# An adjacency product moved into a gap of the q products, and a new order for the first loads and norms

## The chip, the cores and the metric

The kernel runs on one core of one Trainium2 chip. Its time is the device time in microseconds, the median of several runs; the kernel before takes 1536.66 us (1535.83 to 1537.0 in three runs). One more run was profiled; its trace spans 1534.6 us, and every time of a single instruction here is counted from the start of that span.

The engines are named by what they do: TensorE (PE, matmuls; PEld, its weight loads, which can overlap matmuls), VectorE (DVE), ScalarE (ACT), GpSimd (POOL) and SyncE (SP, which here only issues DMA transfers).

## The reference, cut to what matters

128 matrices x of 128 x 512 go through two layers. The first takes the norm of the rows, multiplies by an adjacency matrix and adds the row maximum to x. The second is an attention over 8 heads of 64 with projections q, k and v, in which only pairs count whose adjacency is not zero.

```python
# layer 0
h = jnp.maximum(_layernorm(x, axis=-1), 0.0)
A = jnp.einsum('od,bdn->bon', W1, x)                    # W1 = W2 = adj, x = h
C = jnp.einsum('od,bdn->bon', W2, x) + b[None, :, None]
pre = A[:, :, None, :] + (C - A)[:, :, :, None]
out = jnp.max(jax.nn.relu(pre), axis=-1)                # added to x
# layer 1
h = jnp.maximum(_layernorm(x, axis=-1), 0.0)
q = (x @ Wq + bq).reshape(b, n, H, HD)                  # k and v alike, x = h
scores = jnp.einsum('bihd,bjhd->bhij', q, k) / jnp.sqrt(jnp.float32(HD))
mask = jnp.where(adj == 0, jnp.float32(-1000000000.0), jnp.float32(0.0))
weights = jax.nn.softmax(scores + mask[None, None, :, :], axis=-1)
out = jnp.einsum('bhij,bjhd->bihd', weights, v)         # added to x
```

Because both weights of layer 0 are adj, its output is one number for each row: the maximum of a row of adj @ h, plus a bias, cut at zero. Adding one number to a whole row does not change that row's norm, so the kernel norms each matrix once and uses h in both layers.

## The kernel before

The 128 matrices are worked in 32 groups of four. For each group, q, k and v are formed by a fast matrix product after Strassen and Winograd: seven products (p1 to p7) of half-size blocks of h and of the weights in place of eight. Two of them, p4 and p3, are split once more in the same way (p43a, p43b), except in the first and last group's v. The first group's q is formed in the plain way (`plain_q`). Its results are collected in PSUM banks, read out by ScalarE (`biased`) or added by VectorE.

The norm of one matrix m: statistics on VectorE, two small operations on GpSimd, the rest on ScalarE.

```python
def norm(m):
    ...                                                          # cut: HT, AMAX, C of a new group
    HN[m] = work.tile([P, N], F32, name="hn", bufs=3)
    nc.vector.bn_stats(st, x_of(m))                              # L276
    nc.vector.bn_aggr(mv, st)
    nc.vector.tensor_scalar_add(ve, mv[:, 1:2], EPS)
    nc.gpsimd.tensor_tensor(rstd, ve, mhalf, op=ALU.pow)         # L281
    nc.gpsimd.tensor_scalar(nmr, mv[:, 0:1], rstd, -1.0, op0=ALU.mult, op1=ALU.mult)

def norm_end(m):
    nc.scalar.activation(HN[m], x_of(m), AF.Relu, scale=RSTD[m], bias=NMR[m])   # L286
    if m >= G:
        add_bv(m)                                                # GpSimd, L292
```

h is needed transposed. The first group's four matrices are transposed on TensorE (`transposes`, L318, read out by ScalarE); later ones in 32 x 32 blocks on VectorE (`blocks`, L299), whose blocks 16 small DMA transfers for each pair of matrices then put in place (`move`, L309).

```python
def adjacency(m):
    g, i = divmod(m, G)
    pa = bank(7)
    nc.tensor.matmul(pa, adjT, HN[m], start=True, stop=True)     # L324
    nc.vector.reduce_max(AMAX[g][:, i : i + 1], pa, axis=AX.X)   # L325
    ...                                                          # cut: C of a full group
```

`h_sum` (L342) forms the four sums of blocks of h, `h_blocks` (L351 to L353) and `weight_blocks` (L366) those for the split products, `weight_sums` (L378) those of the weights. The products, cut to what waits for what:

```python
def p1(self):
    self.mm(self.a, "a11", "b11", True)              # eight matmul instructions, L415
    ...                                              # v: one copy on ScalarE
    for f in range(2):
        self.biased(self.pf[f], self.a, f)           # ScalarE, L430: p1a, then u

def p6(self):
    self.mm(self.b, "s2", "t2", True)
    nc.vector.tensor_tensor(self.u[:, 1], self.b, self.pf[0], op=ALU.add)    # L454

def p2(self):
    self.mm(self.a, "a12", "b21")                    # adds into the bank of p1
    self.biased(self.dst(0, 0), self.a, 0)

def p7(self):
    self.mm(self.b, "s3", "t3")                      # adds into the bank of p6
    nc.vector.tensor_tensor(self.u3, self.b, self.pf[1], op=ALU.add)         # L463

def p5(self):
    self.mm(self.c, "s1", "t1", True)
    self.add(self.dst(1, 1), self.c, self.u3)        # L436

def p43b(self):
    for k in range(2):
        self.block_mm(scr[:, 0, k], s[:, k, 2], t[:, k, 2])      # small matmuls, L481
    self.more(u[:, :, 0, 1], scr[:, 0])                          # VectorE, L484
    ...                                                          # cut: 12 instructions into other banks
    for k in range(2):
        self.block_mm(scr[:, 0, k], s[:, k, 1], t[:, k, 1])      # scr again
    ...                                                          # cut: L484 twice, L436 twice
```

The whole is scheduled by hand: each engine works in the order in which its instructions are written. A group's turn is `apply` of the group before (L594), `scores` (L564, read out by ScalarE, L572), then 18 steps: v (steps 0 to 5), q of the next group (6 to 11) and k of the next group (12 to 17), each as p1, p6, p2, (p7, p43a), p5, p43b. After each step other work is put in by a table. `next_norms` is the part for the group after next:

```python
def next_norms(m):
    return {
        0: [(norm_end, m), (norm, m + 1), (norm_end, m + 1)], 4: [(blocks, m)],
        8: [(norm, m + 2), (norm_end, m + 2), (adjacency, m)],
        9: [(blocks, m + 1), (move, m + 1)],
        12: [(norm, m + 3), (norm_end, m + 3), (adjacency, m + 1)],
        13: [(blocks, m + 2)],
        14: [(blocks, m + 3), (move, m + 3), (adjacency, m + 2)],
    }
```

The beginning:

```python
nc.scalar.dma_start(adj_sb, adj)
...
for i in range(G):
    (nc.scalar if i > 0 else nc.sync).dma_start(x_of(i), x[i])
load_w(nc.sync, "q", 0)
load_w(nc.sync, "q", 1)
nc.scalar.activation(live[:, 0:1], mhalf, AF.Copy)
for name in "kv":
    load_w(nc.sync, name, 0)
    load_w(nc.scalar, name, 1)
...                                       # cut: biases on GpSimd's queue, three loads of x, adjT
for m in range(G):
    norm(m)
    norm_end(m)
    if m in (1, 2):
        transposes(m - 1)
    if m == 2:
        adjacency(0)
nc.vector.tensor_single_scalar(live, adjT, 0.0, op=ALU.not_equal)
transposes(2)
adjacency(1)
transposes(3)
adjacency(2)
adjacency(3)
weight_sums(nc.gpsimd, "v")
plain_q(0, 0)
plain_q(0, 1)
weight_sums(nc.vector, "k")
for k in range(4):
    h_sum(0, k)
norm(G); norm_end(G); norm(G + 1); norm_end(G + 1)
plain_q(1, 0)
blocks(G); blocks(G + 1); move(G + 1)
plain_q(1, 1)
...                                       # k of group 0, p1 p6 p2 p7 p5 p4 p3, with other work between
weight_sums(nc.gpsimd, "q")
```

Of the kernel before, what the change touches and what calls it, by code (L numbers as in the profile page):

```python
# [52 lines left out]
P = 128  # L53
G = 4
# [113 lines left out]
def tile_adj_preln_d2(  # L168
# [38 lines left out]
    def fast(ctx):  # L207
# [11 lines left out]
        def bank(k):  # L219

            return ps.tile([P, 512], F32, name=f"bk{k}")

        def x_of(b):
            return X[b // 2][:, b % 2, :]
# [6 lines left out]
        def load_w(eng, name, h):  # L231
            src = dict(q=wq, k=wk, v=wv)[name]
            eng.dma_start(
                W[name][:, 2 * h : 2 * h + 2, :],
                src[2 * h * P : (2 * h + 2) * P].rearrange("(c p) f -> p c f", p=P),
            )
# [3 lines left out]
        for p in range(2):  # L240
            X[p] = xpool.tile([P, 2, N], F32, name="xp")
        for i in range(G):
            (nc.scalar if i > 0 else nc.sync).dma_start(x_of(i), x[i])
        load_w(nc.sync, "q", 0)
        load_w(nc.sync, "q", 1)
        nc.scalar.activation(live[:, 0:1], mhalf, AF.Copy)
        for name in "kv":
            load_w(nc.sync, name, 0)
            load_w(nc.scalar, name, 1)
        nc.gpsimd.dma_start(b0_sb, b0.rearrange("(p o) -> p o", o=1))  # L250
        nc.gpsimd.dma_start(bq_sb, bq.rearrange("(c p) -> p c", p=P), allow_slow_non_contiguous=True)
        nc.gpsimd.dma_start(bk_sb, bk.rearrange("(c p) -> p c", p=P), allow_slow_non_contiguous=True)
# [13 lines left out]
        def norm(m):  # L266

            g, i = divmod(m, G)
            if i == 0:
                HT[g] = proj.tile([P, G, NC, D], F32, name="hT")  # L270
                AMAX[g] = stat.tile([P, G], F32, name="amax")
                C[g] = stat.tile([P, G], F32, name="c")
            HN[m] = work.tile([P, N], F32, name="hn", bufs=3)
            st = stat.tile([P, 6], F32, name="st")
            mv = stat.tile([P, 2], F32, name="mv")
            nc.vector.bn_stats(st, x_of(m))  # L276
            nc.vector.bn_aggr(mv, st)
            ve = stat.tile([P, 1], F32, name="ve")
            nc.vector.tensor_scalar_add(ve, mv[:, 1:2], EPS)  # L279
            rstd = RSTD[m] = stat.tile([P, 1], F32, name="rstd")  # L280
            nc.gpsimd.tensor_tensor(rstd, ve, mhalf, op=ALU.pow)  # L281
            nmr = NMR[m] = stat.tile([P, 1], F32, name="nmr")
            nc.gpsimd.tensor_scalar(nmr, mv[:, 0:1], rstd, -1.0, op0=ALU.mult, op1=ALU.mult)  # L283
# [36 lines left out]

        def adjacency(m):
            g, i = divmod(m, G)
            pa = bank(7)
            nc.tensor.matmul(pa, adjT, HN[m], start=True, stop=True)  # L324
            nc.vector.reduce_max(AMAX[g][:, i : i + 1], pa, axis=AX.X)  # L325
            if i == G - 1:
                nc.vector.tensor_scalar(C[g], AMAX[g], b0_sb, 0.0, op0=ALU.add, op1=ALU.max)
# [54 lines left out]
        def weight_sums(eng, n):  # L382
            for k in range(4):
                weight_sum(eng, n, k)
# [254 lines left out]
        def next_norms(m):  # L639

            return {
                0: [(norm_end, m), (norm, m + 1), (norm_end, m + 1)], 4: [(blocks, m)],
                8: [(norm, m + 2), (norm_end, m + 2), (adjacency, m)],
                9: [(blocks, m + 1), (move, m + 1)],
                12: [(norm, m + 3), (norm_end, m + 3), (adjacency, m + 1)],
                13: [(blocks, m + 2)],
                14: [(blocks, m + 3), (move, m + 3), (adjacency, m + 2)],
            }

        with tc.manual_schedule():  # L650

            for m in range(G):
                norm(m)
                norm_end(m)
                if m in (1, 2):
                    transposes(m - 1)
                if m == 2:
                    adjacency(0)
            nc.vector.tensor_single_scalar(live, adjT, 0.0, op=ALU.not_equal)
            transposes(2)  # L660
            adjacency(1)
            transposes(3)
            adjacency(2)
            adjacency(3)
            weight_sums(nc.gpsimd, "v")
            plain_q(0, 0)
            plain_q(0, 1)
            weight_sums(nc.vector, "k")
            for k in range(4):
                h_sum(0, k)  # L670
            norm(G)
            norm_end(G)
            norm(G + 1)
            norm_end(G + 1)
            plain_q(1, 0)
            blocks(G)
            blocks(G + 1)
            move(G + 1)
            plain_q(1, 1)
            k = Products(0, "k")  # L680
            more = {
                0: [(adjacency, G), (norm, G + 2), (norm_end, G + 2)],
                1: [(norm, G + 3), (norm_end, G + 3), (blocks, G + 2)],
                2: [(adjacency, G + 1)], 3: [(blocks, G + 3), (move, G + 3)],
                4: [(adjacency, G + 2)], 5: [(adjacency, G + 3)],
            }
            for s, p in enumerate((k.p1, k.p6, k.p2, k.p7, k.p5, k.p4, k.p3)):
                p()
                for f, m in more.get(s, ()):
                    f(m)  # L690
            weight_sums(nc.gpsimd, "q")
            for g in range(NG):
                b = g * G
                if g > 0:
                    apply(g - 1)
                scores(g)
                part = []
                for p in [Products(g, "v")] + [Products(g + 1, n) for n in "qk" if g + 1 < NG]:
                    part += [[p.p1], [p.p6], [p.p2]]
                    if p.n == "v" and g in (0, NG - 1):  # L700
                        part += [[p.p7], [p.p5], [p.p4, p.p3]]
                    else:
                        part += [[p.p7, p.p43a], [p.p5], [p.p43b]]
                todo = {s: [] for s in range(len(part))}

                def add(s, *what):
                    todo[s].append(what)

                m = b + 2 * G
                if g + 1 < NG:  # L710
                    if g > 0:
                        for i in range(G):
                            residual(b - G + i)
                    if m < B:
                        norm(m)
                    if 0 < g < NG - 1:
                        add(0, adjacency, m - 1)
                    for k, s in enumerate((1, 2, 2, 3)):
                        add(s if g > 0 else 3, h_sum, g + 1, k)
                    for k, s in enumerate((6, 7)):  # L720
                        add(s, h_blocks, g + 1, k)
                    if g + 2 < NG:
                        for s, l in next_norms(m).items():
                            for what in l:
                                add(s, *what)
                    else:
                        add(6, count, 0, b)
                    eng = nc.gpsimd if m < B else nc.vector
                    for k, s in enumerate((8, 9, 9, 10, 10, 13, 14, 15)):
                        add(s, mask, eng, b + k // 2, k % 2)  # L730
                    if g + 2 < NG:
                        add(0, load, 2 * g + 5)
                    if g + 3 < NG:
                        add(8, load, 2 * g + 6)
                else:
                    for k, s in enumerate((0, 0, 0, 0, 2, 2, 3, 4)):
                        add(s, mask, nc.vector, b + k // 2, k % 2)
                    for i, s in enumerate((0, 0, 0, 1)):
                        add(s, residual, b - G + i)
                if g == 0:  # L740
                    add(0, weight_blocks, nc.gpsimd, "q")
                    add(8, weight_blocks, nc.gpsimd, "k")
                    for i in range(G):
                        add(15, add_bv, i)
                    add(15, weight_blocks, nc.gpsimd, "v")
                for s, ps_ in enumerate(part):
                    for p in ps_:
                        p()
                    for f, *args in todo[s]:
                        f(*args)  # L750

            g = NG - 1
            apply(g, 2)
            count(B - 2 * G, B)
            for i in range(G):
                residual(g * G + i, nc.gpsimd if i < 2 else nc.vector)
            pc = bank(1)
            for k in range(2):
                nc.tensor.matmul(pc[0:1, 0:1], CNT[k], ones, start=k == 0, stop=k == 1)
            nc.scalar.copy(flag, pc[0:1, 0:1])  # L760
# [38 lines left out]
```

## Time and profile before

| engine | busy us | share of the span |
|---|---|---|
| TensorE, matmuls | 1513.8 | 99% |
| TensorE, weight loads | 1322.7 | 86% |
| VectorE | 1158.9 | 76% |
| GpSimd | 600.1 | 39% |
| ScalarE | 426.8 | 28% |

A matmul that stands waiting counts as busy in this table, so 99% does not mean that TensorE is never held up; the spacing of equal pieces of work shows that better. The trace counts matmul instructions as they are executed: a matmul of these 32-bit numbers appears as two, so a product p1 of four matmuls as eight. Back to back the eight take 1.73 us, an adjacency product of two instructions 0.86 us.

The chain of waits is the work that ended last, followed back from the end: a piece of it is work that nothing released later than the piece before. The timeline lists the instructions of all engines in order of time, with the idle time ahead of each and what ended it in brackets.

### The profile page before, as it was taken

Reading aid. Unit: us, or ns where it says so; the run is one execution under the profiler, and the core shown is the slowest. Engines: PE = TensorE matmul, PEld = TensorE weight load, DVE = VectorE, ACT = ScalarE, POOL = GpSimd, SP = SyncE. Lnnn points to the kernel's source line nnn. Section 1 sums busy time; section 2 is a strip of 40 time slices with the busy share of each in tenths; the row PEclk is TensorE's granted clock in tenths of the full one; section 3 lists DMA queues with packets and bytes.
Section 4 is the critical chain, followed back from the end, with each engine's and each line's share of the span. In section 5 each row is a group of like instructions: output and inputs, shape, how many; then the busy total and the mean of one; then the engine's idle time right before and its main releaser. Section 6 shows DMA issues by size and latency. Waiting matters only on the chain.

```text
span 1534.6 us, 32745 instructions
## 1 busy us (share of the span) xinstructions
PE 1513.8 (99%) x12909; PEld 1322.7 (86%) x12909; DVE 1158.9 (76%) x2485; ACT 426.8 (28%) x844; POOL 600.1 (39%) x670
## 2 busy tenths in 40 slices
PE   7999999999999999999999999999999999999997
PEld 5888888888888888888888888888888888888887
DVE  5677777777787777777777877777777777777776
ACT  3223232322232232322322322323223222222221
POOL 4574443243432444423434324344234343243400
PEclk9999999999999999999999999999999999999999
DMA  4233122331222321223312223212233122232111
GB/s 165 51 83 84 26 73 72 81 83 38 65 74 75 84 68 42 72 72 81 84 38 65 72 76 84 62 45 73 73 83 84 29 72 73 77 84 50 44 34 57
DMA packets 307803, 105.28 MB, mean 69 GB/s; under 512 B 273152, under 2 KB 273280, under 8 KB 307648
## 3 DMA queue, kind: packets, MB, share of 16 engines
q1 hardware_dynamic: 306352, 101.00, 25.3%
q8 instruction: 103, 1.69, 0.5%
q10 hardware_dynamic: 1120, 1.90, 0.4%
q14 instruction: 52, 0.43, 0.1%
q0 software_dynamic: 176, 0.27, 0.1%
HBM read 37.03 MB, written 33.55 MB: 46 GB/s over the span
## 4 chain that ended last, share of the span: by engine, by line
PE 97%; DVE 1%; SPq 1%; DMA 1%; issue 0%; POOL 0%; ACT 0%; DVEq 0%; ACTq 0%
PE bk L415 54%; PE bk L481 19%; PE bk L594 8%; PE bk L564 8%; PE bk L324 7%; PE bk L540 1%; SPq L309 1%; DMA xp<-in_x_dram 1%; DVE hs L342 0%; DVE o L612 0%; DVE amax L325 0%; DVE v L436 0%; PE bk L318 0%; ACT hn L286 0%; DVE st L276 0%
## 5 line engine op out<-in xcount | busy, mean ns | idle before, releaser
L281 POOL TENSOR_TENSOR rstd<-ve,mhalf 128x1 f32<-128x1 f32 x128 | 70.7, 552 | 719.4 <-DVE ve L279 719.4
L576 POOL TENSOR_TENSOR w<-w,live 128x512 f32<-128x512 f32 x240 | 297.5, 1272 | 0.0
L484 DVE TENSOR_TENSOR u<-u,bk 128x256 f32<-128x256 f32 x552 | 205.9, 415 | 115.3 <-PE bk L481 111.1
L572 ACT ACTIVATE w<-bk 128x512 f32<-128x512 f32 x256 | 128.9, 624 | 362.7 <-PE bk L564 362.7
L292 POOL TENSOR_TENSOR xp<-xp,bv_sb 128x512 f32<-128x512 f32 x128 | 165.7, 1296 | 118.3 <-ACT hn L286 118.3
L415 PEld LDWEIGHTS bk<-hs,sk_sb 128*128 128x128 f32 x768 | 143.6, 190 | 44.7 <-issue 29.2
L415 PE MATMUL bk<-hs,sk_sb 128*128 128x256 f32 x768 | 181.3, 379 | 0.0
L415 PE MATMUL bk<-sv_sb,hs 128*128 128x256 f32 x768 | 181.2, 379 | 0.0
L415 PE MATMUL bk<-hs,sq_sb 128*128 128x256 f32 x744 | 175.9, 379 | 0.1
L415 PEld LDWEIGHTS bk<-sv_sb,hs 128*128 128x128 f32 x768 | 143.6, 190 | 31.1 <-issue 14.3
L415 PEld LDWEIGHTS bk<-hs,sq_sb 128*128 128x128 f32 x744 | 138.9, 190 | 30.9 <-issue 14.3
L286 ACT ACTIVATE hn<-xp,nmr,rstd 128x512 f32<-128x512 f32 x128 | 104.2, 814 | 161.3 <-POOL nmr L283 161.3
L324 PE MATMUL bk<-hn,adjT 128*128 128x512 f32 x256 | 131.8, 596 | 0.8 <-DVE amax L325 0.8
L463 DVE TENSOR_TENSOR u<-bk,u 128x512 f32<-128x512 f32 x95 | 65.7, 692 | 88.1 <-PE bk L415 85.5
L325 DVE TENSOR_REDUCE amax<-bk 128x1 f32<-128x512 f32 x128 | 88.2, 689 | 52.8 <-PE bk L324 51.9
L594 PE MATMUL bk<-v,w 128*64 128x65 f32 x4096 | 126.6, 222 | 0.0
L594 PEld LDWEIGHTS bk<-v,w 128*64 128x64 f32 x4096 | 122.1, 137 | 4.1 <-issue 0.3
L415 PE MATMUL bk<-wv_sb,hT 128*128 128x256 f32 x512 | 124.3, 386 | 0.0
L564 PE MATMUL bk<-qT,kT 64*128 64x128 f32 x2048 | 122.9, 275 | 0.0
L415 PE MATMUL bk<-hT,wk_sb 128*128 128x256 f32 x512 | 121.1, 379 | 0.0
L415 PE MATMUL bk<-hT,wq_sb 128*128 128x256 f32 x496 | 120.5, 386 | 0.0
L564 PEld LDWEIGHTS bk<-qT,kT 64*128 64x128 f32 x2048 | 116.8, 188 | 2.5 <-issue 0.3
(148 smaller groups left out, 2353.5 us busy)
## 6 DMA issues: line engine op xcount, KB each, us to landing
out_dram<-o SPq DMA_DIRECT2D x128, 256.0 KB, 2.4
xp<-in_x_dram SPq DMA_DIRECT2D x62, 512.0 KB, 4.9
hT<-tb SPq DMA_DIRECT2D x992, 32.0 KB, 1.9
wq_sb<-in_L_gnn_Wq_dram SPq DMA_DIRECT2D x2, 512.0 KB, 6.3
xp<-in_x_dram ACTq DMA_DIRECT2D x3, 256.0 KB, 6.8
wk_sb<-in_L_gnn_Wk_dram SPq DMA_DIRECT2D x1, 512.0 KB, 11.1
wv_sb<-in_L_gnn_Wv_dram SPq DMA_DIRECT2D x1, 512.0 KB, 12.2
wk_sb<-in_L_gnn_Wk_dram ACTq DMA_DIRECT2D x1, 512.0 KB, 9.8
```

What stands on the lines that cost most here:

```text
L281: nc.gpsimd.tensor_tensor(rstd, ve, mhalf, op=ALU.pow)
L286: nc.scalar.activation(HN[m], x_of(m), AF.Relu, scale=RSTD[m], bias=NMR[m])
L292: nc.gpsimd.tensor_tensor(x_m, x_m, bv_sb, op=ALU.add)
L324: nc.tensor.matmul(pa, adjT, HN[m], start=True, stop=True)
L325: nc.vector.reduce_max(AMAX[g][:, i : i + 1], pa, axis=AX.X)
L415: nc.tensor.matmul(bank[:, r, :], lhs, rhs, start=first and r == 0 and c == 0, stop=r == 1 and c == 1, skip_group_check=True,)
L481: nc.tensor.matmul(out, lhs, rhs, start=start, stop=True, skip_group_check=True)
L484: nc.vector.tensor_tensor(to, to, what, op=ALU.add)
L564: nc.tensor.matmul(psc[j][:, f, :], KT[g][r, f, i * D : (i + 1) * D], QT[g][r, f, i * D : (i + 1) * D], start=True, stop=True,)
L572: nc.scalar.activation(w[:, j], psc[j], AF.Exp, scale=HD ** -0.5)
L576: eng.tensor_tensor(w[:, j], w[:, j], live_h, op=ALU.mult)
L594: nc.tensor.matmul(pav[r, c : c + HE], w[:, h % 2, h // 2, r], V[:, i, h, :], start=True, stop=True,)
```

## The change

It moves work; no matmul is added or removed.

- In the turn of a group, the adjacency product of the group after next's first matrix goes from behind q's third product (p2) to between q's second (p6) and third, where p2 has to wait until the bank of p1 has been read out. The block transposition of the same matrix goes from behind v's p5 to behind q's p2.
- At the beginning, the first four matrices and all weights are loaded by one queue, x first. The first group's h is written into the output tile O[0], which is not needed until later, so that four norms need no free hn buffer. Two banks take its adjacency products in turn, and the order of norms, transpositions, adjacency and plain q products is new.
- In group 0 two of the four h sums go two and one steps later, and q's weight blocks are formed ahead of the group's turn. In group 30, the masks that VectorE applies get other steps.

```diff
         for i in range(G):
-            (nc.scalar if i > 0 else nc.sync).dma_start(x_of(i), x[i])
-        load_w(nc.sync, "q", 0)
-        load_w(nc.sync, "q", 1)
+            nc.sync.dma_start(x_of(i), x[i])
         nc.scalar.activation(live[:, 0:1], mhalf, AF.Copy)
-        for name in "kv":
-            load_w(nc.sync, name, 0)
-            load_w(nc.scalar, name, 1)
+        for name in "qkv":
+            for h in range(2):
+                load_w(nc.sync, name, h)
...
-            HN[m] = work.tile([P, N], F32, name="hn", bufs=3)
+            if m < G:
+                if m == 0:
+                    O[0] = one.tile([P, G, N], F32, name="o")
+                HN[m] = O[0][:, m]
+            else:
+                HN[m] = work.tile([P, N], F32, name="hn", bufs=3)
...
-            pa = bank(7)
+            pa = bank(7 if g > 0 else 5 + i % 2)
...
-                0: [(norm_end, m), (norm, m + 1), (norm_end, m + 1)], 4: [(blocks, m)],
-                8: [(norm, m + 2), (norm_end, m + 2), (adjacency, m)],
+                0: [(norm_end, m), (norm, m + 1), (norm_end, m + 1)],
+                7: [(adjacency, m)], 8: [(norm, m + 2), (norm_end, m + 2), (blocks, m)],
...
             for m in range(G):
                 norm(m)
-                norm_end(m)
-                if m in (1, 2):
-                    transposes(m - 1)
-                if m == 2:
-                    adjacency(0)
+                if m < 2:
+                    norm_end(m)
+            transposes(0)
+            transposes(1)
+            norm_end(2)
+            norm_end(3)
             nc.vector.tensor_single_scalar(live, adjT, 0.0, op=ALU.not_equal)
+            adjacency(0)
+            adjacency(1)
             transposes(2)
-            adjacency(1)
             transposes(3)
-            adjacency(2)
-            adjacency(3)
             weight_sums(nc.gpsimd, "v")
             plain_q(0, 0)
+            adjacency(2)
             plain_q(0, 1)
+            adjacency(3)
             weight_sums(nc.vector, "k")
...
             weight_sums(nc.gpsimd, "q")
+            weight_blocks(nc.gpsimd, "q")
...
-                    for k, s in enumerate((1, 2, 2, 3)):
-                        add(s if g > 0 else 3, h_sum, g + 1, k)
+                    for k, s in enumerate((1, 2, 2, 3) if g > 0 else (3, 3, 4, 5)):
+                        add(s, h_sum, g + 1, k)
...
-                    for k, s in enumerate((8, 9, 9, 10, 10, 13, 14, 15)):
+                    at = (8, 9, 9, 10, 10, 13, 14, 15) if m < B else (4, 8, 8, 12, 12, 13, 14, 14)
+                    for k, s in enumerate(at):
                         add(s, mask, eng, b + k // 2, k % 2)
...
-                    add(0, weight_blocks, nc.gpsimd, "q")
```

## The prediction

> **What bounds the kernel now.** I read the page first, for the engine that is full and for the chain that ended last.
>
> ```profile
> PE 1513.8 (99%) x12909; PEld 1322.7 (86%) x12909; DVE 1158.9 (76%) x2485; ACT 426.8 (28%) x844; POOL 600.1 (39%) x670
> PE 97%; DVE 1%; SPq 1%; DMA 1%; issue 0%; POOL 0%; ACT 0%; DVEq 0%; ACTq 0%
> ```
>
> TensorE sets the end nearly everywhere, at a clock granted at nine tenths or more in all 40 slices. The change removes no matmul, so all it can win is time in which TensorE waits. The list of waits shows little of that under PE, but one entry under the weight loads comes back in every group of four matrices:
>
> ```profile
> PEld bk L415 <- ACT u L430: 12.5, 32, 0.4
> ```
>
> (engine, line, what it waited for: us in total, times, longest). Because busy time includes a matmul that stands waiting for its weights, I then took the chain of waits piece by piece, for a late, undisturbed group (start, duration, what):
>
> ```profile
> 1419.03 5.18 PE bk L415 x24
> ...
> 1426.83 2.42 PE bk L481 x20
> 1429.25 5.45 PE bk L415 x24
> 1434.70 0.86 PE bk L324 x2
> ...
> 1439.90 2.23 PE bk L481 x20
> ```
>
> Equal work takes unequal time here. Twenty-four instructions of products one to three take 5.18 us, but 5.45 for q. Twenty small ones of the split products take 2.23 for q and k, but 2.42 for v. So q's first three products lose 0.26 us (5.44 or 5.45 against 5.18; I take 0.26) and v's small products 0.19 us in each group. The chain shows the same pair of excesses throughout, group after group, 47.02 us apart (236.95, 283.97, 330.98 for the score products). The timeline of the same group shows the two causes:
>
> ```profile
> 1427.48 0.70 DVE L299 STREAM_TRANSPOSE tb<-hn 128x512 f32<-128x512 f32 x1
> ...
> 1428.10 0.38 DVE L484 TENSOR_TENSOR u<-u,bk 128x256 f32<-128x256 f32 x1
> ...
> 1428.54 0.71 PE L481 MATMUL bk<-ssv_sb,h 128*128 128x128 f32 x4
> ...
> 1431.81 0.85 ACT L430 ACTIVATE u<-bk,bq_sb 128x256 f32<-128x256 f32 x2
> ...
> 1432.70 1.59 PEld L415 LDWEIGHTS bk<-hT,wq_sb 128*128 128x128 f32 x8 [0.40 <-ACT u L430]
> ```
>
> The block transposition (L299) stands on VectorE ahead of the addition L484, which has to empty the scratch bank before v's last four small matmuls may write it: L484 ends at 1428.48, they start at 1428.54. In q the third product adds into the first product's bank, which ScalarE is still reading out into p1a and u; it is done at 1432.66.
>
> For the beginning I read the timeline from 0 to 48 us. From 18.39 us on TensorE works without a break (13.81 us of plain q products, then k's products and four adjacencies) to the score products at 47.66. What stands close behind it is this row of ScalarE work:
>
> ```profile
> 31.56 0.81 ACT L286 ACTIVATE hn<-xp,nmr,rstd 128x512 f32<-128x512 f32 x1 [2.25 <-POOL nmr L283]
> ...
> 32.27 1.55 ACT L547 ACTIVATE qT<-bk,bq_sb 128x256 f32<-128x256 f32 x4
> ...
> 34.70 0.84 ACT L430 ACTIVATE u<-bk,bk_sb 128x256 f32<-128x256 f32 x2
> ...
> 36.36 1.89 PE L415 MATMUL bk<-hT,wk_sb 128*128 128x256 f32 x8
> ```
>
> ScalarE ends u at 35.54, and k's third product starts at 36.36: only 0.8 us of slack. Last, the v products of group 0:
>
> ```profile
> 62.66 0.68 DVE L436 TENSOR_TENSOR v<-bk,u 128x512 f32<-128x512 f32 x1
> ...
> 63.48 1.96 PE L415 MATMUL bk<-sv_sb,hT 128*128 128x256 f32 x8 [1.42 <-DVE v L436]
> ```
>
> **What the Trainium skill says.** "TensorE: Matmul & The Clock Gate", section "Step-by-step: what each phase is for": the queue of TensorE pulls weight loads ahead of running matmuls, the matmuls stay in order. The trace agrees: the loads of a product normally begin 0.2 us before its first matmul; at q's third product they begin with it (1432.70 and 1432.71). Same page, "What's actually happening": the array begins at half clock and is released by activity. Four transpositions take 1.11 us at 6.92 and 0.66 at 11.51. "DMA: Bandwidth & Descriptors", "Issuing engines are not separate DMA queues": transfers of all issuers share the same 16 engines. The trace moves 315 to 406 GB/s in the late slices of the first 20 us, when little but SyncE's own loads is left, so I take one queue to be no slower. "SBUF — State Buffer", "Who interferes with whom": a VectorE instruction with two SBUF inputs and a GpSimd one that reads SBUF block each other. Here such a sum takes 1.64 us instead of 0.68 (at 21.08, beside GpSimd's sums).
>
> **The change, part by part.**
>
> 1. Adjacency between q's second and third product, in groups 0 to 29. The 0.86 us of adjacency is only moved. It starts when the second product ends, about 257.0 in the group I worked on; ScalarE is done with u at 257.12, the third product now starts at 257.9. The wait goes: 30 x 0.26 = 7.8 us.
>
> 2. The block transposition moves from v's fifth product to behind q's third. VectorE then reaches L484 as soon as the matmuls before it end. Groups 1 to 29 (group 0 has no small v products): 29 x 0.19 = 5.5 us. Does it make a wait in its new place? There VectorE must do, from the end of q's second product: L454 0.60 (pitch), h sums 1.0, amax 0.6, statistics 1.0, transposition 0.65, together some 4 us, and is then due at L463 when the fourth product ends. TensorE takes 0.86 + 1.73 + 1.73 = 4.3 us until then. It just fits; before, VectorE stood idle 1.10 us there. I count 0.
>
> 3. Group 0, v: L436 stood behind four h sums. With two of them moved back it can end near 61.1, before the fourth product ends (60.17 + 1.73 = 61.90). The last product starts there instead of 63.48, that is 1.58; I count 1.5.
>
> 4. Group 0, k: before the small k products the chain shows 2.50 us for the twenty instead of 2.23, behind a row hn - add bv - masks and weight blocks on GpSimd - statistics - hn. Part 1 and 2 move amax ahead of the statistics (0.66 us later), while TensorE comes 0.26 earlier. I expect 0.9 us more waiting there, once. Elsewhere GpSimd has 0.5 us of idle time at that place and takes it up.
>
> 5. Group 30: masks on VectorE. q's small products are torn apart there, from 1486.22 to 1489.72 in place of 2.23 us: 1.27 lost. The new places free them, but one mask now stands where the transposition stood in v (0.19). Gain 1.1.
>
> 6. The beginning. All of x goes first, about 1.1 MB with adj; at 0.4 MB per us after some 2.5 us x3 lands near 5.7 (the third and fourth norm started at 8.52 and 11.98 before). The norms then follow each other on VectorE at 1.0 us, ScalarE finishes hn of matrix 3 near 11.2, and TensorE runs from 6.92 with little rest: two cold transpositions 2.2, a cold adjacency 1.7, a warm one 0.9, two transpositions 0.9. The plain q products start near 12.6 instead of 18.39. But two adjacencies now lie between them, VectorE does the k weight sums and h sums only after the fourth amax, and that starts at 12.6 + 2 x (3.45 + 0.86) = 21.2. Then 6.0 us to the norm of matrix 4 (7.94 before, less 1.9 for the collision with GpSimd's sums, which now come earlier), 5.19 to hn of matrix 5 (26.37 to 31.56 before) and 3.7 until ScalarE is done with u (31.56 to 35.54, less 0.25 of waiting for TensorE). k's third product then starts at 36.2, against 36.36. TensorE wins almost 6 us at the start and hands it back in two waits around k's first three products. I count 0.1.
>
> The weight blocks of q on GpSimd end near 51 instead of 64 us; q's second small use of them was not waited for, so nothing. Sum: 7.8 + 5.5 + 1.5 - 0.9 + 1.1 + 0.1 = 15.1 us, 1536.66 - 15.1 = 1521.6.
>
> **The rivals.** (a) The transposition makes a wait of its own behind q's third product, since it fits by only some 0.3 us; VectorE's 76% speak for it, its idle 1.10 us against it. A wait like v's would come back: 30 x 0.19 = 5.7 us lost, 1527.3. (b) The beginning does bring its gain, if VectorE's sums are faster or the plain products start earlier than I think: up to 3.6 us at k's first product (18.39 + 13.81 = 32.20 against 12.6 + 13.81 + 1.72 = 28.1, were nothing else late), so 1518. Against it stands the row of ScalarE shown above. (c) The output tile serves four norms and is followed as one thing: then the first transposition waits for hn of matrix 1 and the first adjacency for hn of matrix 3, the plain products start near 14, and k's third product 1.4 us later than now: 1523. (d) Moving the adjacency moves a wait to q's fourth product, which needs L454: it ends 257.98, and the product starts 259.6. Nothing speaks for it.
>
> **Range and chances.** The two gains per group are read off identical pieces of the trace and are the surest: 13.3 us. The single places add up to 1.8 with an uncertainty of about 3 either way, and rival (a) costs up to 6. So 1517.5 to 1527.5 holds it 8 times in 10. For 2% some 30.7 us would have to go; all waits together don't hold as much. Chances: faster by over 2% 0.02, within 2% 0.97, slower 0.01.
>
> **What would show it.** The distance from one group's score products to the next should fall from 47.02 to 46.57 us; q's three products should read 1.73 + 1.73, an adjacency of 0.86, then 1.73, and v's twenty 2.23. The weight loads' wait for u should drop from 32 entries to two or so. Plain q should start near 12.6, k's third product near 36.2 with a wait for ScalarE ahead of it. A 2.42 in q's twenty would show (a); k's third product at 34 would show (b). If groups stay at 47.02 the reading of the pieces is wrong.

## The result, and the profile after

| | median us | range | runs |
|---|---|---|---|
| before | 1536.55 | 1535.83 to 1537.0 | 5 |
| after | 1521.13 | 1520.77 to 1521.34 | 5 |

The ratio is 0.99, with a 95% interval of 0.9885 to 0.9914: 15.4 us less. The profiled span fell by as much, from 1534.6 to 1519.2 us. First the page of the changed kernel: busy time by engine, then the chain that ended last, by engine.

```profile
PE 1499.8 (99%) x12909; PEld 1323.4 (87%) x12909; DVE 1152.1 (76%) x2485; ACT 426.6 (28%) x844; POOL 597.3 (39%) x670
PE 96%; DVE 2%; POOL 1%; ACT 0%; issue 0%; DMA 0%; DVEq 0%; POOLq 0%; ACTq 0%
```

The number of matmuls is the same, 12909, yet TensorE's busy time fell by 14.0 us. A matmul that waits counts as busy, so nearly the whole gain is waiting that had been hidden in this figure. The list of waits (us in total, times, longest) shows it for the weight loads; before, this entry stood at 32 times:

```profile
PEld bk L418 <- ACT u L433: 4.2, 3, 3.5
```

Line numbers are three higher than before: L418 is the products, L484 the small matmuls, L327 the adjacency. The chain of waits for the same group (start, duration, what; v, then q, then k):

```profile
1412.95 2.23 PE bk L484 x20
1415.18 3.46 PE bk L418 x16
1418.64 0.86 PE bk L327 x2
1419.49 3.45 PE bk L418 x16
...
1425.57 2.23 PE bk L484 x20
```

v's twenty small matmuls take 2.23 us in place of 2.42. q's first two products take 3.46, the adjacency 0.86, and the next two products 3.45: no piece is longer than its like elsewhere. From one group's score products to the next it is 46.57 us (234.40 to 280.96), before 47.02.

The beginning, from the timeline (start, duration, engine, line, tiles, shape; in brackets the idle time ahead and what ended it):

```profile
12.38 3.62 PE L543 MATMUL bk<-hT,wq_sb 128*128 128x256 f32 x16
```

```profile
32.32 0.81 ACT L289 ACTIVATE hn<-xp,nmr,rstd 128x512 f32<-128x512 f32 x1 [2.26 <-POOL nmr L286]
33.04 1.56 ACT L550 ACTIVATE qT<-bk,bq_sb 128x256 f32<-128x256 f32 x4
...
35.18 0.87 ACT L433 ACTIVATE u<-bk,bk_sb 128x256 f32<-128x256 f32 x2
...
36.11 1.99 PE L418 MATMUL bk<-hT,wk_sb 128*128 128x256 f32 x8 [3.14 <-ACT u L433]
```

The plain q products start 5.85 us earlier than before (in the chain of waits at 12.54, against 18.39), and k's third product 0.25 us earlier: TensorE now stands 3.14 us waiting for the row on ScalarE, which in turn waited 2.26 for GpSimd's end of a norm (nmr).

**Where the 15.4 us came from**, read from the starts of score and apply products in both chains:

| stretch | gain us |
|---|---|
| to the scores of group 0 | 0.14 |
| the rest of group 0's turn | 1.06 |
| groups 1 to 29, 29 x 0.453 | 13.14 |
| group 30 | 1.07 |

### The profile page after: what moved, and what is told of

Same layout as the page of the kernel before. It is cut to its first block, busy times and chain, and to the rows that moved or that the text cites. A ratio compares the mean times of both kernels' runs of the same rounds, so it can differ in the third digit from the quotient of the medians.

```text
span 1519.2 us, 32776 instructions
## 1 busy us (share of the span) xinstructions
PE 1499.8 (99%) x12909; PEld 1323.4 (87%) x12909; DVE 1152.1 (76%) x2485; ACT 426.6 (28%) x844; POOL 597.3 (39%) x670
## 4 chain that ended last, share of the span: by engine, by line
PE 96%; DVE 2%; POOL 1%; ACT 0%; issue 0%; DMA 0%; DVEq 0%; POOLq 0%; ACTq 0%
PE bk L418 54%; PE bk L484 19%; PE bk L597 8%; PE bk L567 8%; PE bk L327 7%; PE bk L543 0%; POOL w L579 0%; POOL ssk_sb L369 0%; PE bk L321 0%; DMA xp<-in_x_dram 0%; POOL rstd L284 0%; DVE sk_sb L381 0%; POOL xp L295 0%; DVE hs L345 0%; ACT hn L289 0%
## 5 line engine op out<-in xcount | busy, mean ns | idle before, releaser
L418 PEld LDWEIGHTS bk<-hs,sk_sb 128*128 128x128 f32 x768 | 143.6, 190 | 44.7 <-issue 29.2
L418 PE MATMUL bk<-hs,sk_sb 128*128 128x256 f32 x768 | 181.3, 379 | 0.0
L418 PE MATMUL bk<-sv_sb,hs 128*128 128x256 f32 x768 | 181.2, 379 | 0.0
L418 PE MATMUL bk<-hs,sq_sb 128*128 128x256 f32 x744 | 175.9, 379 | 0.1
L418 PEld LDWEIGHTS bk<-sv_sb,hs 128*128 128x128 f32 x768 | 143.6, 190 | 31.1 <-issue 14.3
L418 PEld LDWEIGHTS bk<-hs,sq_sb 128*128 128x128 f32 x744 | 138.9, 190 | 18.1 <-DVE u L457 0.5
L289 ACT ACTIVATE hn<-xp,nmr,rstd 128x512 f32<-128x512 f32 x124 | 100.9, 814 | 169.1 <-POOL nmr L286 169.0
L327 PE MATMUL bk<-hn,adjT 128*128 128x512 f32 x248 | 126.7, 592 | 0.3 <-ACT hn L289 0.3
L418 PE MATMUL bk<-hT,wk_sb 128*128 128x256 f32 x512 | 121.2, 380 | 3.1 <-ACT u L433 3.1
L418 PE MATMUL bk<-wv_sb,hT 128*128 128x256 f32 x512 | 124.3, 386 | 0.0
L418 PE MATMUL bk<-hT,wq_sb 128*128 128x256 f32 x496 | 117.3, 379 | 0.0
```

The lines of the kernel that those rows point to most:

```text
L418: nc.tensor.matmul(bank[:, r, :], lhs, rhs, start=first and r == 0 and c == 0, stop=r == 1 and c == 1, skip_group_check=True,)
```

## The experiments

The theory: the gain per group is two separate waits of TensorE (for ScalarE's u in q, for VectorE's transposition in v), the beginning gives nothing, and two single places give the rest. The rivals: the beginning does take part in the gain; the two moves need each other; the transposition sits in its new place with no room left.

**The adjacency alone** (before, with the product moved to step 7 and the transposition left in v):

```diff
-                8: [(norm, m + 2), (norm_end, m + 2), (adjacency, m)],
+                7: [(adjacency, m)], 8: [(norm, m + 2), (norm_end, m + 2)],
```

> The kernel before, with the adjacency product alone moved between q's second and third product; the block transposition stays behind v's fifth. My theory (two separate waits): 30 x 0.26 = 7.8 us faster, less 0.7 to 0.9 in group 0 where the statistics move behind the row maximum, so about 1529.6; q's first three products spaced 1.73, 1.73, 0.86, 1.73, v's twenty small matmuls still 2.42. Rival one (both excesses have one cause, the place of the adjacency product): some 12.5 us faster, v's twenty at 2.23. Rival two (what costs is the switch between kinds of products, not the wait): no change, 1536.5.

Measured: 1529.65 us (1529.54 to 1529.89; before on that chip 1536.45), ratio 0.9956, 0.9942 to 0.9969. A group takes 46.75 us, 0.26 less. Its chain (v, then q):

```profile
1374.01 2.42 PE bk L481 x20
1376.43 3.46 PE bk L415 x16
1379.88 0.86 PE bk L324 x2
1380.74 3.45 PE bk L415 x16
```

q's excess is gone, v's 2.42 stays. The moved product removes q's wait by itself and nothing else. In group 0 k's small products wait 0.98 us here (0.18 before), the one cost that was predicted for it.

**The transposition alone** (before, `blocks` at the end of step 8, the adjacency left there):

```diff
-                0: [(norm_end, m), (norm, m + 1), (norm_end, m + 1)], 4: [(blocks, m)],
-                8: [(norm, m + 2), (norm_end, m + 2), (adjacency, m)],
+                0: [(norm_end, m), (norm, m + 1), (norm_end, m + 1)],
+                8: [(norm, m + 2), (norm_end, m + 2), (adjacency, m), (blocks, m)],
```

> The kernel before, with the block transposition alone moved from behind v's fifth to behind q's third product; the adjacency product stays behind q's third. My theory: 29 x 0.19 = 5.5 us faster, about 1531.0; v's twenty small matmuls 2.23, the three q products still 5.44. Rival (the transposition brings its wait along to q): nothing won, v 2.23 but q's twenty 2.42, 1536.5.

Measured: 1531.12 us (1530.74 to 1531.42), ratio 0.9965, 0.9951 to 0.9979; 46.83 us a group, 0.19 less. The mirror image in the chain:

```profile
1375.11 2.23 PE bk L481 x20
1377.34 5.44 PE bk L415 x24
```

0.26 and 0.19 make the 0.45 us that the whole change brings: the two add up, and neither needs the other.

**The beginning alone** (before, with the one queue, the norms into the output tile, the two banks and the new order of the start; nothing else).

> The kernel before, with the new beginning alone (one queue, first h in the output tile, two banks, new order up to the plain q products); groups are worked as before. My theory (the gain is handed back in the wait for ScalarE ahead of k's third product): plain q starts near 12.4 instead of 18.2, k's third product near 36.1 instead of 36.4, time 0.2 us less, 1536.4. Rival (the beginning brings what its plain products win): 3.6 to 5.8 us faster, 1531 to 1533.

Measured: 1537.23 us (1535.61 to 1539.85), ratio 1.0007, 0.9999 to 1.0015: no gain. Its timeline shows the same pair of rows as the changed kernel, a start at 12.38 and a wait that takes it back:

```profile
12.38 3.62 PE L543 MATMUL bk<-hT,wq_sb 128*128 128x256 f32 x16
...
36.12 1.99 PE L418 MATMUL bk<-hT,wk_sb 128*128 128x256 f32 x8 [3.14 <-ACT u L433]
```

v's last product of group 0 still starts 1.59 us after the end of the one before it, so that gain isn't part of the beginning either.

**Two queues again** (after, with the x and weight loads divided between SyncE and ScalarE as before). It asks what the single queue is worth when the start around it is the new one.

```diff
-            nc.sync.dma_start(x_of(i), x[i])
+            (nc.scalar if i > 0 else nc.sync).dma_start(x_of(i), x[i])
+        load_w(nc.sync, "q", 0)
+        load_w(nc.sync, "q", 1)
...
+            load_w(nc.scalar, name, 1)
```

> The changed kernel, with the loads on two queues again as before. My theory: the third and fourth norm start 2 to 4 us later, plain q starts 0.5 to 2 us later, and since the fourth row maximum, the sums and the norm of matrix 4 follow it one for one, k's third product and the end are as much later: 1521.6 to 1523.1. Rival (the loads were never on the way, only the order of work was): no change, 1521.1.

Measured: 1525.15 us (1524.07 to 1525.34), ratio 0.9927, 0.9913 to 0.994; the span is 3.1 us longer than after. The profiled run is the fastest of the five; the other four take another 1 us, and what that is stays open. The third matrix's statistics wait for their data, and everything behind follows:

```profile
10.02 0.69 DVE L281 BATCH_NORM_STATS2 st<-xp 128x6 f32<-128x512 f32 x1 [3.21 <-DMA xp<-in_x_dram]
```

```profile
39.03 1.99 PE L420 MATMUL bk<-hT,wk_sb 128*128 128x256 f32 x8 [3.13 <-ACT u L435]
```

The plain q products start at 15.31 (2.93 later) and k's third product at 39.03 (2.92 later), behind the same wait of 3.13. So the wait does not absorb a later start: the row that k's third product waits for begins at the plain q products, and moves with them. The expectation had this part right (all behind the plain q products follows one for one), but put their delay at only 0.5 to 2 us. With the new order of the start the single queue is worth 3 us: on two queues k's third product comes 2.7 us later than in the kernel before (39.03 against 36.36). The run does not separate the number of queues from the order of the loads: on two queues q's weights move beside x (the three x on ScalarE's queue take 8.3 us to land in the median, the four on the single queue 3.8), and two queues with all of x first were not tried.

**Transposed twice, and three times** (after, with the transposition of step 8 repeated into the same tile, once and twice). This measures the room that VectorE has in its new place, which the prediction put at 0.3 us.

```diff
-                ... (norm_end, m + 2), (blocks, m)],
+                ... (norm_end, m + 2), (blocks, m), (again, m)],               # twice
+                ... (norm_end, m + 2), (blocks, m), (again, m), (again, m)],   # three times
```

> The changed kernel, with the block transposition behind q's third product done twice (0.65 us more on VectorE in 30 groups, same result written again). Reading of the trace of the changed kernel: VectorE stands idle 0.34 us ahead of L466 and about 0.2 us ahead of L487, so L487 ends only 0.1 us later and 0.2 us before TensorE needs the scratch bank: no change, 1521.1. My prediction's reading (it fits by some 0.3 us): a wait of 0.2 to 0.35 us in each group, 6 to 10 us slower, 1527 to 1531.

Measured: 1524.56 us (1522.73 to 1524.88; before 1536.27), ratio 0.9919, 0.9903 to 0.9936. A group takes 46.62 us, 0.06 more: 1.7 us in all. The chain has the loss in q's twenty small matmuls, which take 2.23 after:

```profile
1382.76 2.28 PE bk L490 x20
```

The rest lies in the beginning: 0.7 us ahead of k's third product (36.80 against 36.11), which stays open, and 1.4 between it and the scores of group 0 (last section).

> The changed kernel, with that transposition done three times (1.3 us more on VectorE). Reading of its trace: L466 0.96 us later, the end of L487 0.75 us later, past the point where TensorE needs the scratch bank by 0.35 to 0.5 us: 30 x 0.35 to 0.5 = 10 to 15 us slower, 1531 to 1536, q's twenty small matmuls 2.6 to 2.7 instead of 2.23. If VectorE has slack that I don't see (it catches up later): no change.

Measured: 1547.51 us (1545.49 to 1548.31), ratio 1.0074, 1.0058 to 1.0091: 11 us slower than before. A group takes 47.37 us, 0.80 more than after. The waits of TensorE and, for one group, the chain from q's products on:

```profile
PE bk L490 <- DVE u L493: 14.2, 30, 0.8
```

```profile
1349.56 0.61 DVE st L279
...
1350.63 0.63 DVE tb L302
1351.29 0.72 DVE tb L308
...
1352.67 0.66 DVE u L472
...
1353.42 1.09 DVE u L493 x3
...
1354.56 2.58 PE bk L490 x20
```

The chain runs through VectorE here: statistics, transposition, its repeats (the first at L308, the second in the gap listed as issue), then the additions that TensorE waits for. Each repeat costs VectorE 0.73 us (two take 1.46). Two repeats lost 0.80, one 0.06: both give a room of 0.66 us (1.46 - 0.80, and 0.73 - 0.06 = 0.67), twice the predicted 0.3.

Two waits share that loss. With one repeat the small matmuls still start on time, 6.08 us behind the start of q's third product (6.07 after). The 0.06 are lost inside the twenty: a weight load there starts 0.28 us behind the one before it, not 0.22, just after the addition of q's fifth product (L445) has ended and set its bank free. With two repeats 0.62 us are lost ahead of the twenty (6.69 in place of 6.07) and 0.18 inside them.

The changed kernel's own timeline shows the room ahead of the twenty:

```profile
257.81 0.70 DVE L302 STREAM_TRANSPOSE tb<-hn 128x512 f32<-128x512 f32 x1
...
258.85 0.69 DVE L466 TENSOR_TENSOR u<-bk,u 128x512 f32<-128x512 f32 x1 [0.34 <-PE bk L418]
...
259.68 1.08 DVE L487 TENSOR_TENSOR u<-u,bk 128x256 f32<-128x256 f32 x3
...
261.20 0.61 PE L484 MATMUL bk<-h,ssq_sb 128*128 128x128 f32 x4
```

VectorE stands idle 0.34 us for q's fourth product, which is the 0.3 that was foreseen. But being late there costs TensorE nothing until the three additions behind it end later than the scratch bank is wanted: they end at 260.76, the small matmuls start at 261.20, another 0.44 us. The two make 0.78, more than the measured 0.66, since the fifth product's addition is late first.

**The h sums of group 0 left together** (after, with all four in step 3). Is v's gain in group 0 the new place of the sums, or q's weight blocks, which no longer run on GpSimd beside them?

```diff
-                    for k, s in enumerate((1, 2, 2, 3) if g > 0 else (3, 3, 4, 5)):
+                    for k, s in enumerate((1, 2, 2, 3) if g > 0 else (3, 3, 3, 3)):
```

> The changed kernel, with group 0's four h sums all behind v's fourth product again. My theory: v's last product of group 0 starts some 1.1 to 1.6 us later; that moves the end by as much unless the wait in k of group 0 (0.98 us) swallows it, because that wait is behind GpSimd's work that starts from the same VectorE row: 0.2 to 1.5 us slower, 1521.3 to 1522.6. Rival (GpSimd's weight blocks made the sums long, and they are elsewhere now): no wait, 1521.1.

Measured: 1522.15 us (1521.72 to 1524.58), ratio 0.9907, 0.989 to 0.9923. The last product is due at 64.03 and starts here:

```profile
64.74 1.97 PE L418 MATMUL bk<-sv_sb,hT 128*128 128x256 f32 x8 [0.55 <-DVE v L439]
```

0.71 us of the 1.58 come back. The other 0.87 are the sums themselves: four of them take 2.53 us here (61.39 to 63.92) and took 3.41 before (59.25 to 62.66), when GpSimd formed the weight blocks at the same time.

**The weight blocks back in the turn** (after, with q's weight blocks in step 0 of group 0 again, the h sums left apart).

```diff
             weight_sums(nc.gpsimd, "q")
-            weight_blocks(nc.gpsimd, "q")
...
+                    add(0, weight_blocks, nc.gpsimd, "q")
```

> The changed kernel, with q's weight blocks on GpSimd back in group 0's turn. My theory: VectorE's h sums beside them stretch from 0.6 to about 0.9 us each, but only two stand ahead of v's fifth addition, so it ends near 61.6, before the fourth product does (61.7): no change, 1521.1. Rival (of the 1.58 us that v's last product waited before, the port shared with GpSimd made the larger part, and the new place of the h sums the smaller): 0.5 to 0.9 us slower, 1521.6 to 1522.0.

Measured: 1523.12 us (1521.57 to 1524.39), ratio 0.9905, 0.9889 to 0.9922. The h sums are slowed again (0.89 and 0.83 in place of 0.68), but v's last product comes without a wait, 1.72 us after the one before it, at 64.85. So moving the sums apart is enough by itself, with the blocks or without; moving the blocks away alone leaves 0.71. The profiled run's span is 3.2 us longer than after's, but not from this place: 2.9 of it lie between k's third product and the scores of group 0 (last section).

**The norms of matrices 4 and 5 earlier** (after, the two norms moved from behind the k sums to behind the third adjacency). The changed kernel waits 3.14 us for the row that begins with them.

```diff
             adjacency(2)
+            for m in (G, G + 1):
+                norm(m)
+                norm_end(m)
             plain_q(0, 1)
...
-            norm(G)
-            norm_end(G)
-            norm(G + 1)
-            norm_end(G + 1)
```

> The changed kernel, with the norms of matrices 4 and 5 worked behind the third adjacency product, ahead of the k weight sums and h sums. My theory (k's third product waits for ScalarE, which waits for this row): k's third product starts at 32.2 instead of 36.1, no wait ahead of it, and all that follows moves up: 3.9 us faster than the changed kernel, about 1517.2. Rival (another wait takes its place, on VectorE's sums or on the block transfers that fill h of group 1): at most 1 us faster, 1520 to 1521.

Measured: 1518.5 us (1517.66 to 1519.47), ratio 0.9882, 0.9866 to 0.9899. k's third product starts at 34.05, only 2.06 us earlier, and two waits are left:

```profile
31.13 1.99 PE L418 MATMUL bk<-hs,sk_sb 128*128 128x256 f32 x8 [0.70 <-ACT qT L550]
34.05 1.99 PE L418 MATMUL bk<-hT,wk_sb 128*128 128x256 f32 x8 [0.93 <-ACT u L433]
```

GpSimd's timeline shows why: the first small step of the norm stands behind four of its sums for v, which waited for v's weights until 18.28, and takes twice its 0.55 us beside VectorE's k sums.

```profile
22.08 1.27 POOL L381 TENSOR_TENSOR sv_sb<-wv_sb,sv_sb 128x512 f32<-128x512 f32 x1
23.30 1.07 POOL L284 TENSOR_TENSOR rstd<-ve,mhalf 128x1 f32<-128x1 f32 x1
```

**The norms ahead of GpSimd's sums** (the last kernel, with the v sums moved behind the two norms too).

```diff
-            weight_sums(nc.gpsimd, "v")
             plain_q(0, 0)
             adjacency(2)
+            for m in (G, G + 1):
+                norm(m)
+                norm_end(m)
+            weight_sums(nc.gpsimd, "v")
             plain_q(0, 1)
```

> As the kernel with the norms of matrices 4 and 5 moved ahead, and GpSimd's v weight sums now behind those norms instead of in front. My theory (what was left of the wait ahead of k's third product, 0.70 and 0.93 us, came from GpSimd: its v sums waited for their weights, and then shared its port with VectorE's k sums): k's third product starts at 32.0 to 32.3, the score products of group 0 at 43.5, 4.0 us faster than the changed kernel, about 1517.0. Rival (the two norms' GpSimd work is slow wherever it stands, or the v sums now slow VectorE's k and h sums as much): k's third product at 33.5 to 34.5 again, 1518.5.

Measured: 1517.74 us (1517.09 to 1519.6; before 1536.48), ratio 0.9876, 0.986 to 0.9893. The wait is gone:

```profile
32.46 1.89 PE L418 MATMUL bk<-hT,wk_sb 128*128 128x256 f32 x8
```

k's third product starts 3.65 us earlier than after, and the scores of group 0 at 43.76, 3.76 earlier; the span is 3.4 us shorter. So the early start of the plain q products is worth something once the row behind them is brought forward as well.

**Further** (the last kernel, with k's weight blocks formed ahead of the groups, and in group 30 the masks on VectorE and the count in other steps).

```diff
             weight_blocks(nc.gpsimd, "q")
+            weight_blocks(nc.gpsimd, "k")
...
-                        add(6, count, 0, b)
+                        add(11, count, 0, b)
...
-                    at = ... if m < B else (4, 8, 8, 12, 12, 13, 14, 14)
+                    at = ... if m < B else (8, 8, 8, 13, 13, 14, 14, 14)
...
-                    add(8, weight_blocks, nc.gpsimd, "k")
```

> The same, and k's weight blocks formed ahead of group 0's turn, and in group 30 no mask behind v's fifth product and the count moved behind q's products. My theory: the wait in k of group 0 (0.98 us and 0.27 us in its twenty small matmuls) goes, since GpSimd's row there gets 3.3 us shorter; group 30's v loses its 0.2 us, its q the 0.3 us ahead of the fourth product: 1.7 us faster than the kernel with only the norms moved, about 1515.3. Rival (the row through GpSimd is bound by the masks as well): 0.5 us, 1516.5.

Measured: 1516.62 us (1515.59 to 1516.94), ratio 0.9867, 0.9851 to 0.9884; the span is 5.5 us shorter than after. It is the fastest of all. The chain, by engine, and group 0's small k products in it:

```profile
PE 99%; DVE 0%; DMA 0%; POOL 0%; ACT 0%; DVEq 0%; issue 0%
```

```profile
83.41 2.23 PE bk L484 x20
```

k's twenty took 2.50 us behind a wait of 0.98 in the changed kernel. It comes 1.3 us later than expected: 0.7 of that the kernel it starts from was short of its own expectation (1517.74 against 1517.0), and the other 0.6 stay open. The profiled run, the fastest of the four, has a span 2.1 us shorter than that kernel's, more than the 1.7 expected.

## Why the prediction held

1521.6 us was predicted and 1521.13 measured. Point by point:

1. **The adjacency in q**: 0.26 us a group predicted, 0.26 measured when it stands alone.
2. **The transposition**: 0.19 predicted and measured. That it makes no wait in its new place was right; that it "fits by only some 0.3 us" was mis-sized. The term left out is the room behind the fourth product's addition: with the 0.34 of idle time ahead of it the whole room is 0.66, as measured by repeating the transposition. So rival (a) was further off than stated.
3. **v of group 0**: 1.5 counted; the wait it was read from, 1.58, is gone. The cause named, the sums' place, is enough for it by itself. What the prediction did not see is that the blocks' new place, which it gave nothing, would have brought 0.87 of it had the sums stayed.
4. **k of group 0**: 0.9 more waiting predicted. The small products start 0.98 us behind the product before them, 0.18 before: 0.80 more. The wait belongs to the adjacency's move, as said: with the adjacency alone it is 0.98 as well, with the transposition alone the products start as in the kernel before.
5. **Group 30**: 1.1 predicted, 1.07 measured. v's twenty became 2.44 there, as foreseen, and q's 2.23.
6. **The beginning**: 0.1 predicted, 0.14 measured, with 12.38 and 36.11 us where 12.6 and 36.2 were predicted. The steps between fit as well: the fourth row maximum starts at 21.20 (21.2 predicted) and the norm of matrix 4 at 27.13 (27.2), so the small number is not luck. One reading was wrong: the 315 to 406 GB/s were not little but SyncE's loads, since ScalarE's halves of the k and v weights landed only near 13.8 and 16.5 us. The conclusion stood: the single queue moves 388 to 409 GB/s from 10 to 18 us. Rival (b) did not happen. Its 3.6 should have been 4.1 by its own figures (32.20 less 28.1), and k's first product does start 4.1 us earlier (27.91 against 32.04), but nothing of it reaches the end. The run with the norms ahead of the sums, whose scores of group 0 come 3.76 earlier, shows that (b) was held back by the row the prediction named. Rival (c) did not show: the first transposition starts at 6.70, ahead of the end of matrix 1's h (6.82 to 7.63). Nor did (d): no wait stands at q's fourth product.

The sum agrees within 0.3 us, and no two errors had to cancel for it: the largest of a single term is some 0.1 us. Two expectations written later were undersized. Two queues were expected to delay the plain q products by 0.5 to 2 us, and delayed them by 2.93. Three transpositions were expected to lose 0.35 to 0.5 us a group, and lost 0.80: a repeat was taken at 0.65 us and costs 0.73, and a second wait inside the twenty was not seen.

## What to carry to other kernels

An engine at 99% can still be waiting: compare equal pieces of work in the chain and count how often the longer one comes back, since 0.26 and 0.19 us in 30 groups were worth 13 us, while almost 6 us won at the start were worth 0.14. A start brought forward pays only as far as the next row that it doesn't bring forward, so follow that row to its first instruction (here the statistics of a norm behind eight sums on VectorE, and once these were moved, a one-element-wide step of the norm behind four sums on GpSimd). To learn how much room an instruction has, repeat it once and twice: here the second repeat cost 0.74 us a group for 0.73 us of work, so the room was used up by then, while the idle time beside the instruction showed only the part up to the next wait.

## What was not expected of the hardware

In three of the profiled runs TensorE's granted clock fell to half at or behind the 3.1 us wait ahead of k's third product: with the transposition twice, with the h sums together, and with the weight blocks back. In four others with the same wait (after, the beginning alone, two queues, three transpositions) it did not. The same stretches of after and of the run with the weight blocks back (stretch, us, busy PE, PEld, DVE, ACT, POOL with their counts, granted clock, DMA share, GB/s):

```profile
36.00:41.00 5.00, 4.89 (x21) 3.95 (x22) 2.75 (x7) 2.25 (x5) 2.94 (x6) 1.00 0.31 52
```

```profile
36.00:41.00 5.00, 4.66 (x10) 3.40 (x11) 2.02 (x5) 2.25 (x5) 2.94 (x6) 0.50 0.31 52
41.00:46.00 5.00, 5.00 (x19) 3.73 (x19) 2.45 (x4) 0.38 (x2) 4.92 (x5) 0.88 0.28 46
```

In five microseconds TensorE does 10 matmuls in place of 21. The products show it one by one:

```profile
36.34 3.78 PE L418 MATMUL bk<-hT,wk_sb 128*128 128x256 f32 x8 [3.14 <-ACT u L433]
```

3.78 us is twice the usual 1.89. From here to the scores of group 0 it takes 14.28 us (36.34 to 50.62), after 11.41 (36.11 to 47.52): 2.9 us, though the work is the same. With the transposition twice the clock was 0.66 in this stretch, with the h sums together 0.70.

Read in steps of 0.1 us, the clock goes from 1.00 to 0.50 at 35.36 us with the weight blocks back and at 36.25 with the transposition twice, 2.2 and 2.6 us after the matmuls ahead of the wait had ended. With the h sums together it goes only at 38.01, when k's third product has been running at full clock for 1.3 us: the spacing of its instructions doubles there from 0.21 to 0.43 us. It stays at 0.50 for 6.83, 3.41 and 3.41 us.

The Trainium skill, "TensorE: Matmul & The Clock Gate", section "What's actually happening", says that the array drops to half clock after an idle window of about 3.4 us, and that the window runs freely. The 3.41 us and their double agree with such a window. That all of it must be idle does not come out here: in the 3.41 us ahead of the three drops TensorE worked for 1.2, 0.8 and 1.3 us (the runs in the order of the last paragraph), and stood idle for 2.2, 2.6 and 2.1. So waits shorter than the window lost the clock in three of seven profiled runs. Why not in the other four is not shown: where the windows lie does not appear in the traces. The spread of 4.2 us in the beginning alone may come from the same thing, but its one profiled run has no drop. The two kernels without the wait, the norms ahead of the sums and the one after it, have a clock of 1.00 in all stretches from 32 to 46 us.
